# Byte offsets for fetched rows from VectorE, three tiles of five, and a run of 19 slices

## The chip, the cores and the metric

The kernel runs on one core of a Trainium2 chip. The metric is the device time of one execution in microseconds. A core has five engines that run their own instruction streams in order: TensorE (PE, whose weight loads the profile lists apart as PEld), VectorE (DVE), ScalarE (ACT), GpSimd (POOL) and SyncE (SP). They meet at semaphores. Sixteen DMA engines move data between the chip's memory (DRAM) and the on-chip buffers; in this kernel SP and POOL issue all transfers.

## The reference

A recommendation model: for each of 16384 samples, rows of tables are looked up and averaged, and three dense layers follow.

```
tok = word_emb[token_idx].mean(axis=1)          # 32 lookups in a 50000 x 300 table
e1 = emb_mh1[mh1_idx].mean(axis=1)              # 20 lookups each in tables of
e2 = emb_mh2[mh2_idx].mean(axis=1)              # 1000, 5000 and 10000 rows of 64
e3 = emb_mh3[mh3_idx].mean(axis=1)
o1, o2, o3, o4 = emb_oh1[oh1_idx], ...          # one lookup each, 100, 50, 20, 1000 rows
emb = concatenate([tok, e1, e2, e3, o1, o2, o3, o4], axis=1)
wide = sum of the looked-up rows of the seven width-1 tables
h = relu(emb @ W1 + b1)                         # 748 -> 1024
h = relu(h @ W2 + b2)                           # -> 512
h = relu(h @ W3 + b3)                           # -> 256
return sigmoid(h @ Wd + bd + wide)
```

All tensors are float32.

## The kernel before

**Tiles and steps.** The samples are cut into 128 tiles of 128 samples, one sample a partition. The program is one long list, written out by a loop over steps (lines 710 to 791): 11 steps a tile, and 27 more (`WAKE`) at the end, 1435 in all. In each step the loop issues a share of every kind of work, and each engine runs its own part of the list in the order in which it was issued. So the order of the work on every engine is fixed by hand; the engines only wait for each other's data and buffers.

**Small tables by counting.** The seven small tables (with their width-1 columns beside them) are not gathered. They stay on chip as 138 slices of 128 rows (`terms`): 8 for e1, 8 for o4, 40 for e2, 79 for e3 and one each for o1, o2, o3. For a tile, `one_hots` (line 387, DVE, then ACT) and `counts` (line 404, PE, then ACT) make a count of how often each sample names each row (`cnt`); the counts of tile t are made in the 11 steps of tile t. In the steps of the next tile, `small_sums` (line 427) multiplies each of the 138 slices of counts by its slice of the tables (line 447, PE). The fields go in pairs, (e1, o4), (e2, e3), (o1, o2) and (o3) alone: 16, 119, 2 and 1 slices. A pair's sums stand in the one bank `pg` (a pool with `bufs=1`, line 124), and a DVE reduction (line 437) empties it into the tile's features `g`. The next pair's first product waits for that reduction.

How many slices a step takes is a table made at lines 636 to 643. `early_sums` are issued ahead of the step's layer work, `late_sums` after it. Before the change they are 16 in step 1 (early), 20 in step 2 (late), 20 in each of steps 3 to 7 (early), 2 in step 9 (early) and 1 in step 10 (late). `run_sums` (line 647) draws that many from the generator, whatever pair they belong to, and `flush` (line 653) issues the reductions that have become due at the end of the step; a reduction of an early run is due in its own step, of a late run one step later. `sums_done` is the running total, and the layers are paced by how far it is from an even share (`ahead`, line 769).

**Word rows.** Each sample needs 32 rows of the word table, 1200 bytes each. `tokens` (line 285) issues an indirect gather on POOL for each of the 32 positions (line 300), two to a group, into one of six `tok_rows` buffers; three groups later `add_up` (line 272) adds both rows to a running sum on DVE (lines 276, 278 and 283). The groups are spread evenly over the steps, 1.42 groups (2.84 positions) a step after the first 24.

For some tiles the last of the 32 positions is not gathered by POOL. `load_column` (line 313) has SP load the tile's 128 indices of that position into one partition. `fetch` (line 320) has SP read them into its registers, 16 at a time (line 326), and issue one DMA a row (line 335), 128 rows a tile, into a buffer `fetched`, from which the last addition reads (line 283). Which tiles these are is line 679: every second one from tile 4. A fetch begins 24 steps before the step in which its tile is summed up (`FETCH_AHEAD`) and its rows are spread over 20 steps; the column is loaded 4 steps before that. `fetched` and `column` have two buffers each.

**Layers.** Two steps after a tile's features are complete they are transposed (line 488, PE; line 492, DVE) into `x`. Blocks of three tiles (two and one near the end) run through the three layers (line 565, PE; line 576, ACT) piece by piece within the steps, and the output is stored by SP (line 609).

**Order within a step**, as far as the change touches it: one-hots of the next step, counts, early sums, column loads and fetches, word-row groups, layers, late sums, then the reductions due.

Of the kernel before, what the change touches and what calls it, by code (L numbers as in the profile page):

```python
# [8 lines left out]
F32 = mybir.dt.float32  # L9
# [2 lines left out]
I32 = mybir.dt.int32  # L12
U32 = mybir.dt.uint32
U16 = mybir.dt.uint16
AF = mybir.ActivationFunctionType
ALU = mybir.AluOpType
AX = mybir.AxisListType

P = 128
N_TOK, TOK_D = 32, 300  # L20
# [7 lines left out]
FETCH_FROM = 4  # L28
FETCH_STEPS = 20
FETCH_AHEAD = 24  # L30
COLUMN_AHEAD = 4
LOADS = 16
WAKE = 27
EARLY = 3
BLOCK = 256
# [39 lines left out]
def kernel(  # L75
# [21 lines left out]
    nc = tc.nc  # L97
# [7 lines left out]
    for f in SMALL:  # L105
        n = -(-tables[f].shape[0] // P)
# [10 lines left out]
    fp = ctx.enter_context(tc.tile_pool(name="fetched", bufs=2))  # L117
# [54 lines left out]
    at = 0  # L172
# [27 lines left out]
    def convert_tables():  # L200
# [11 lines left out]
        def term(p, c):  # L212
            _, a, b = pieces[p]
            return terms[:, a:b, c * ROW : (c + 1) * ROW]

        def rows(p):
            k, a, b = pieces[p]
            return raws[k][:, a - parts[k] : b - parts[k], :]

        def make(p, c):  # L220

            if c == 0:
                nc.scalar.activation(term(p, 0), rows(p), AF.Copy, scale=COUNT)
                return
# [3 lines left out]
            for k in range(c):  # L228
                nc.tensor.matmul(left, minus_count, term(p, k), start=False, stop=(k == c - 1))
            nc.scalar.activation(term(p, c), left, AF.Copy, scale=COUNT)  # L230

# [77 lines left out]
            yield 1  # L309

    fetched, columns = {}, {}

    def load_column(t):

        columns[t] = fp.tile([1, P], I32, name="column")
        nc.sync.dma_start(
            out=columns[t], in_=idx[t * P : (t + 1) * P, N_TOK - 1 : N_TOK].rearrange("n o -> o n")
        )

    def fetch(t):  # L320


        rows = fp.tile([P, TOK_D], F32, name="fetched")
        column = columns.pop(t)
        for p0 in range(0, P, LOADS):
            _, values = nc.values_load_multi_w_load_instructions(
                column[:, p0 : p0 + LOADS],
                engines=[mybir.EngineType.SP],
                min_val=0,
                max_val=word.shape[0] - 1,  # L330
                skip_runtime_bounds_check_because="the indices are rows of the table",
            )
            for i, value in enumerate(values):
                p = p0 + i
                nc.sync.dma_start(out=rows[p : p + 1, :], in_=word[bass.ds(value, 1), :])  # L335
                if p == P - 1:
                    fetched[t] = rows
                yield 1

    def load_indices(blk):  # L340
# [46 lines left out]
    def one_hots(sc, s, i):  # L387
# [12 lines left out]
        upper = hot.rearrange("p (k w) n -> p k w n", w=2)[HALF:P, 0:rows, 0, 0:P]  # L400
        nc.scalar.activation(upper, upper, AF.Copy, scale=UPPER)  # L401
        return hot

    def counts(cnt, hot, i):
# [5 lines left out]
        for k in range(rows):  # L410
# [6 lines left out]
            pc[:, :, 0 : n * n_h].rearrange("l g (k h) -> l h g k", h=n_h),  # L417
            AF.Copy,
        )
# [122 lines left out]
    def flush_outputs():  # L542
        while pending:
            pending.pop(0)()
# [5 lines left out]
    def layer(dst, weights, bias, srcs, n_out, part=None):  # L550
# [3 lines left out]
        for m in range(n_out):  # L554
# [20 lines left out]
            def evict(m=m, ph=ph):  # L575
                nc.scalar.activation(dst[:, m, 0:n], ph[:, 0:n], AF.Relu, bias=bias[:, m : m + 1])  # L576

# [3 lines left out]
    def mlp(block, part=None):  # L581
# [20 lines left out]
        def finish():  # L602
            y = block.wide()
            nc.vector.tensor_add(y, po[:, 0:n].rearrange("o (a b) -> o a b", b=P), y)
            nc.scalar.activation(y, y, AF.Sigmoid, bias=bd_sb)
            b0 = block.first * P
# [29 lines left out]
    n_of = {f: slices[f][1] - slices[f][0] for f in SMALL}  # L636
    sizes_of_pairs = [sum(n_of[f] for f in SMALL[i : i + 2]) for i in (0, 2, 4, 6)]
    large = -(-sizes_of_pairs[1] // 6)
    early_sums = {1: sizes_of_pairs[0], 9: sizes_of_pairs[2], **{i: large for i in range(3, 8)}}
    late_sums = {2: large, 10: sizes_of_pairs[3]}  # L640
    sums_done = [0]
    for i in range(STEPS):
# [4 lines left out]
    def run_sums(gen, n, step, due):  # L647
        for _ in range(n):
            evict = next(gen, None)
            if evict:  # L650
                later.append((due, evict))
# [8 lines left out]
    tiles = B // P  # L660
    n_steps = tiles * STEPS + WAKE
    mlp_work = NK * M1 + M1 * M2 + M2 * M3 + M3
# [11 lines left out]
    def summed_at(t):  # L674

        n = n_groups * (t + 1) + TOK_LAG
        return n / FRONT_PACE if n < front else FRONT_STEPS + (n - front) / pace

    fetches = [(int(summed_at(t)) - FETCH_AHEAD, t) for t in range(FETCH_FROM, tiles, 2)]
    fetching = []  # L680

    def speed(step):

        left = n_steps - step
        return 1 / (TILE_STEPS if left > WAKE else TILE_STEPS_SUMS if left > STEPS + EARLY else TILE_STEPS_LAST)

# [6 lines left out]
    def block_for(t):  # L693
        if t not in block_of:
            n = ends[t] - t
            block = Block(t, n)
            block_of.update({t + k: block for k in range(n)})
        return block_of[t]
# [11 lines left out]
    for step in range(n_steps):  # L710
        t, i = divmod(step, STEPS)
        s = t % NSUB
        blk = t // NSUB + 1
        more = blk * NSUB < tiles
        if i == 0:
            sums = small_sums(t - 1, cnt) if 1 <= t <= tiles else None
            if t < tiles:
                if s == 0 and t:
                    sc = next_sc
                cnt = cp.tile([P, n_h, HALF], U16, name="cnt", tag="counts")  # L720
        if t < tiles:
            hot_now = hot
            if more and s == 0 and i == 0:
                ix = load_indices(blk)
            if more and s == 0 and i == 8:
                next_keys = lookup_keys(ix)
            if i < STEPS - 1:
                hot = one_hots(sc, s, i + 1)
            elif t + 1 < tiles:
                hot = one_hots(next_sc if s == NSUB - 1 else sc, (s + 1) % NSUB, 0)  # L730
            flush_outputs()
            counts(cnt, hot_now, i)
            tables_on_chip.to(TABLE_PACE * (step - 2))
            if t == 1 and i == STEPS - 1:
                load_weights()
        else:
            flush_outputs()
        if sums:
            run_sums(sums, early_sums.get(i, 0), step, step)
        outputs = list(rows_out)  # L740
        if waiting and step >= waiting[0][0]:
            _, k, ks = waiting[0]
            if k in summed or ks[0] < N_EARLY and k == tiles - 1:
                waiting.pop(0)
                block = block_for(k)
                later.append((step, block.transpose(k, ks)))
                if not block.missing:
                    complete.append(block)
        if complete and layers is None:
            flush(step)  # L750
            block = complete.pop(0)
            layers, target = start(block), 0
        for at, t_f in fetches:
            if step == at - COLUMN_AHEAD:
                load_column(t_f)
            if step == at:
                fetching.append((at, Paced(fetch(t_f))))
        for at, rows in list(fetching):
            rows.to(P * (step + 1 - at) / FETCH_STEPS)
            if step + 1 - at >= FETCH_STEPS:  # L760
                rows.finish()
                fetching.remove((at, rows))
        toks.to(tokens_by(step + 1))
        if t < tiles and more and s == 1 and i == (5 if t > 1 else 9):
            next_sc, evict = key_columns(next_keys)
            later.append((step, evict))
        ahead = 0
        if sums:
            ahead = n_h * (i + 1) / STEPS - sums_done[i + 1]
        if layers:  # L770
            target += mlp_work * LAYER_TIME * speed(step)
            layers.to(target + ahead)
            if layers.done >= layers.total:
                layers.finish()
                target -= layers.total
                layers = start(complete.pop(0)) if complete else None
        if sums:
            run_sums(sums, late_sums.get(i, 0), step, step + 1)
        flush(step)
        if outputs and rows_out[: len(outputs)] == outputs:  # L780
            flush_rows()
        flush_stores()
        if i == 0 and 2 <= t <= tiles + 1:
            wide_term(features(t - 2))
            if t - 2 < tiles - 1:
                waiting.append((step + 2, t - 2, range(NK)))
            else:
                waiting.append((step + 1, t - 2, range(N_EARLY)))
                waiting.append((step + 2, t - 2, range(N_EARLY, NK)))
        if step == n_steps - EARLY:  # L790
            part = early_part(block_of[tiles - 1])
# [49 lines left out]
```

## Time and profile before

| | us |
|---|---|
| runs: median (lowest to highest) | 5163.98 (5158.36 to 5164.18) |
| the profiled execution | 5157.98 |
| its span, first to last instruction | 5156.2 |
| PE busy | 4809.1 |
| POOL busy | 3819.6 |
| DVE busy | 3754.0 |
| ACT busy | 2757.7 |
| word gathers on POOL (line 300), 4034 | 3818.7 |
| slices on PE (line 447), 17664 | 1735.9 |
| reductions of `pg` on DVE (line 437), 512 | 262.1 |
| SP waiting for outputs to store (line 609), 51 times | 833.6 |

The profile is of one execution. Busy times are sums over an engine's instructions; register and DMA-issuing instructions count as busy on no engine, so SP has no busy share, and its load is read from the times between its instructions. Matmuls are pipelined, and their listed lengths overlap: the 17664 slices have a mean length of 248 ns, while 20 in a row take 1.9 us.

A line of groups gives the source line, the engine, the operation, what it writes and reads, and how often; then busy time and mean length; then how long the engine stood idle just ahead of it, and what ended that. A line of waits gives who waited for whom, the sum in us, how many times, and the longest. A line of the timeline gives the start in us, the length, engine and line, and in brackets the idle time before it with its releaser. "issue" means that nothing which the profile shows was waited for. A lane of DVE or ACT is one partition.

### The profile page before, as it was taken

To read this page: it belongs to the slowest core of one execution; us is meant where nothing else is said; L and a number is where in the kernel's file an instruction comes from. 1 tells how busy PE (TensorE), PEld (TensorE's weight loads), DVE (VectorE), ACT (ScalarE), POOL (GpSimd) and SP (SyncE) were. 2 spreads that over 40 slices of the span, in tenths; PEclk is the share of its full clock that TensorE was granted. 3 is DMA by queue.
4 is the path that set the end of the run, shared out by engine and by line. 5 is a ranking of instruction groups with operands and counts; after the bars stand their busy time and mean duration, and the time that the engine had idled before them with its cause. 6 is when DMAs were issued, how large, how long until landed. Compare 5 with 4: busy or idle time off the path is not lost.

```text
span 5156.2 us, 119649 instructions
## 1 busy us (share of the span) xinstructions
PE 4809.1 (93%) x36252; PEld 3716.6 (72%) x36252; DVE 3754.0 (73%) x6664; ACT 2757.7 (53%) x3658; POOL 3819.6 (74%) x4041
## 2 busy tenths in 40 slices
PE   6799999999999999999999999999999999999999
PEld 4566676676676667666667766766767888888898
DVE  6777777777777777777777777777777777777774
ACT  6455555555555555555555555555555555555552
POOL 7777777777777777777777777777777777777775
PEclk8899999999999999999999999999999999999999
DMA  7444444444444444444444444444444444444443
GB/s 202 128 126 126 123 127 127 124 126 124 125 127 123 124 127 124 125 126 125 125 125 126 125 126 123 127 128 127 127 128 124 126 125 124 128 127 127 127 120 100
DMA packets 276178, 653.78 MB, mean 127 GB/s; under 512 B 136091, under 2 KB 144667, under 8 KB 275527
## 3 DMA queue, kind: packets, MB, share of 16 engines
q0 software_dynamic: 193632, 619.88, 44.4%
q1 hardware_dynamic: 81895, 26.25, 2.4%
q8 instruction: 283, 4.64, 0.4%
q14 instruction: 368, 3.01, 0.2%
HBM read 645.63 MB, written 0.07 MB: 125 GB/s over the span
## 4 chain that ended last, share of the span: by engine, by line
PE 83%; DVE 9%; DMA 3%; issue 2%; ACT 2%; POOL 1%; SPq 1%; DVEq 0%; POOLq 0%; ACTq 0%
PE ph L565 44%; PE pg L447 28%; PE pc L412 8%; DMA tok_rows<-in_word_emb_dram,it 3%; DVE g L437 2%; DVE hot L394 2%; DVE own L278 2%; DVE own L283 2%; PE pc L488 2%; POOL tok_rows L300 1%; PE po L597 1%; DVE x L492 1%; ACT cnt L415 1%; ACT hot L401 0%; SPq L335 0%
## 5 line engine op out<-in xcount | busy, mean ns | idle before, releaser
L300 POOL DMA_INDIRECT tok_rows<-in_word_emb_dram,it x4034 | 3818.7, 947 | 1309.7 <-issue 907.9
L447 PE MATMUL pg<-terms,cnt 128*128 128x195 bf16 x17664 | 1735.9, 248 | 206.1 <-DVE g L437 206.1
L401 ACT ACTIVATE hot<-hot 64x768 bf16<-64x768 bf16 (+1 forms) x1408 | 1155.4, 821 | 1443.4 <-DVE hot L394 1427.5
L394 DVE TENSOR_TENSOR hot<-own,sc 128x1656 bf16<-128x1656 bf16 (+1 forms) x1408 | 1393.5, 990 | 367.9 <-PE pc L412 306.3
L447 PEld LDWEIGHTS <-cnt 128*128 128x128 fp8e3 x17664 | 1520.7, 98 | 43.2 <-issue 26.7
L565 PE MATMUL ph<-x,w_sb 128*128 128x384 f32 (+5 forms) x4932 | 1489.6, 441 | 45.8 <-DVE x L492 44.9
L415 ACT ACTIVATE cnt<-pc 128x828 uint16<-128x828 f32 (+1 forms) x1408 | 1186.9, 843 | 642.2 <-PE pc L412 615.0
L565 PE MATMUL ph<-h,w_sb 128*128 128x384 f32 (+2 forms) x4160 | 1219.6, 433 | 0.0
L565 PEld LDWEIGHTS ph<-x,w_sb 128*128 128x128 f32 (+1 forms) x4932 | 839.7, 192 | 454.9 <-issue 102.7
L278 DVE TENSOR_TENSOR own<-own,tok_rows 128x300 f32<-128x300 f32 x1920 | 917.5, 478 | 82.9 <-DMA tok_rows<-in_word_emb_dram,it 18.6
L565 PEld LDWEIGHTS ph<-h,w_sb 128*128 128x128 f32 x4160 | 700.4, 190 | 351.5 <-issue 103.8
L412 PEld LDWEIGHTS <-hot 128*128 128x128 bf16 x8192 | 592.0, 98 | 466.4 <-issue 220.7
L283 DVE TENSOR_TENSOR own<-own,tok_rows 128x300 f32<-128x300 f32 x1792 | 856.6, 478 | 94.3 <-DMA tok_rows<-in_word_emb_dram,it 33.3
L412 PE MATMUL pc<-hot 128*128 128x138 bf16 x8192 | 727.9, 224 | 55.8 <-ACT hot L401 53.5
L437 DVE TENSOR_REDUCE g<-pg 128x130 f32<-128x390 f32 (+1 forms) x512 | 262.1, 512 | 523.6 <-PE pg L447 518.2
L576 ACT ACTIVATE h<-ph,b_sb 128x384 f32<-128x384 f32 (+2 forms) x723 | 378.8, 524 | 274.6 <-PE ph L565 263.9
L492 DVE TENSOR_TENSOR x<-pc,scale 128x768 f32<-128x768 f32 x127 | 120.8, 951 | 105.8 <-PE pc L488 105.4
L381 DVE COPY sc<-pc 128x512 bf16<-128x512 bf16 x64 | 44.2, 691 | 144.4 <-PE pc L377 139.0
L488 PE MATMUL pc<-ident,g 128*128 128x128 f32 x762 | 106.7, 277 | 9.9 <-ACT cnt L415 9.9
L488 PEld LDWEIGHTS pc<-ident,g 128*128 128x128 f32 x762 | 83.0, 142 | 21.1 <-ACT cnt L415 16.8
L597 PE MATMUL po<-h,wd_sb 128*1 128x384 f32 (+2 forms) x208 | 70.0, 426 | 4.0 <-ACT h L576 2.7
L276 DVE TENSOR_TENSOR own<-tok_rows 128x300 f32<-128x300 f32 x128 | 61.3, 479 | 7.6 <-DMA tok_rows<-in_word_emb_dram,it 3.7
(54 smaller groups left out, 397.0 us busy)
## 6 DMA issues: line engine op xcount, KB each, us to landing
fetched<-in_word_emb_dram SPq DMA_DIRECT2D x7936, 1.2 KB
tok_rows<-in_word_emb_dram,it POOLq DMA_INDIRECT x4034
ix<-in_idx_dram SPq DMA_DIRECT2D x128, 32.0 KB
w_sb<-in_W_dram SPq DMA_DIRECT2D x6, 512.0 KB
raw<-in_mh_dram SPq DMA_DIRECT2D x4, 682.5 KB
it<-in_idx_dram SPq DMA_DIRECT2D x64, 32.0 KB
w_sb<-in_W_dram SPq DMA_DIRECT2D x1, 2048.0 KB
column<-in_idx_dram SPq DMA_DIRECT2D x62, 0.5 KB
```

The lines of the kernel that those rows point to most:

```text
L278: nc.vector.tensor_add(tok_sum, tok_sum, a)
L283: nc.vector.tensor_add(to, tok_sum, b)
L300: nc.gpsimd.indirect_dma_start(out=rows[-1], out_offset=None, in_=word, in_offset=bass.IndirectOffsetOnAxis(ap=it[:, j : j + 1], axis=0),)
L394: nc.vector.tensor_tensor(hot[:, 0 : 2 * rows, :].rearrange("p i (n d) -> p i n d", d=2), iota.rearrange("p (n d) -> p n d", d=2).unsqueez ...
L401: nc.scalar.activation(upper, upper, AF.Copy, scale=UPPER)
L412: nc.tensor.matmul(pc[:, k // n, at : at + n_h], hot[:, 2 * k, 0:P], hot[:, 2 * k + 1, :], start=True, stop=True)
L415: nc.scalar.activation(cnt[:, :, b : b + rows].rearrange("l h (g k) -> l h g k", g=2), pc[:, :, 0 : n * n_h].rearrange("l g (k h) -> l h g ...
L437: nc.vector.tensor_reduce(field_columns(features(t), pair), pg[:, 0:n, :].rearrange("p f (c d) -> p f d c", c=3), AX.X, ALU.add,)
L447: nc.tensor.matmul(pg[:, j, :], by_slice[:, h, :], terms[:, h, :], start=(h == h0), stop=(h == h1 - 1))
L488: nc.tensor.transpose(pt[:, j // n, j % n, :], g[:, c : c + P], ident)
L565: nc.tensor.matmul(to, weights[: src.shape[0], k, m * P : (m + 1) * P], src, start=(k == 0), stop=(k == len(srcs) - 1),)
L576: nc.scalar.activation(dst[:, m, 0:n], ph[:, 0:n], AF.Relu, bias=bias[:, m : m + 1])
```

## The change

Three things change.

1. The indices of a fetched column are turned into byte offsets on DVE. A new function `column_offsets` multiplies the 128 indices by 75 and shifts them left by 4 bits (together 1200, the bytes of a row), in place, one step before the fetch begins. The word table and the `fetched` buffer are seen as bytes, so the value that SP loads into a register is the offset of the DMA as it stands. According to the change's description SP then has one instruction a row.
2. The fetched tiles are those with t mod 5 equal to 0, 2 or 4, from tile 4 on: 75 tiles instead of 62.
3. The sixth run of the second pair (step 7) has 119 - 5 x 20 = 19 slices instead of 20. With that, step 9 holds o1 and o2, and step 10 holds o3, issued after the layers of that step, its reduction one step later.

```diff
+COLUMN_LAG = 1
 LOADS = 16
+ROW_BYTES = 4 * TOK_D
...
     fetched, columns = {}, {}
+    word_bytes = word.bitcast(U8).rearrange("n d -> (n d)").unsqueeze(0)
...
+    def column_offsets(t):
+
+
+        column = columns[t]
+        low = ROW_BYTES & -ROW_BYTES
+        nc.vector.tensor_single_scalar(column, column, ROW_BYTES // low, op=ALU.mult)
+        nc.vector.tensor_single_scalar(column, column, low.bit_length() - 1, op=ALU.logical_shift_left)
+
     def fetch(t):
...
-        rows = fp.tile([P, TOK_D], F32, name="fetched")
+        rows = fp.tile([P, TOK_D], F32, name="fetched").bitcast(U8)
...
-                max_val=word.shape[0] - 1,
+                max_val=(word.shape[0] - 1) * ROW_BYTES,
...
-                nc.sync.dma_start(out=rows[p : p + 1, :], in_=word[bass.ds(value, 1), :])
+                nc.sync.dma_start(out=rows[p : p + 1, :], in_=word_bytes[:, bass.ds(value, ROW_BYTES)])
                 if p == P - 1:
-                    fetched[t] = rows
+                    fetched[t] = rows.bitcast(F32)
...
-    early_sums = {1: sizes_of_pairs[0], 9: sizes_of_pairs[2], **{i: large for i in range(3, 8)}}
+    early_sums = {1: sizes_of_pairs[0], 9: sizes_of_pairs[2], **{i: large for i in range(3, 7)}}
+    early_sums[7] = sizes_of_pairs[1] - 5 * large
...
-    fetches = [(int(summed_at(t)) - FETCH_AHEAD, t) for t in range(FETCH_FROM, tiles, 2)]
+    fetches = [(int(summed_at(t)) - FETCH_AHEAD, t) for t in range(FETCH_FROM, tiles) if t % 5 % 2 == 0]
...
         for at, t_f in fetches:
             if step == at - COLUMN_AHEAD:
                 load_column(t_f)
+            if step == at - COLUMN_LAG:
+                column_offsets(t_f)
             if step == at:
                 fetching.append((at, Paced(fetch(t_f))))
```

More of the change, by code (lines that the diff above doesn't have):

```diff
@@ L14 @@
 U16 = mybir.dt.uint16
+U8 = mybir.dt.uint8
 AF = mybir.ActivationFunctionType
```

## The prediction

> **What bounds the kernel now.** I read the busy shares first, then what TensorE (PE) waits for, then the gathers' group on GpSimd (POOL), then the timeline of one tile.
>
> The page's first part and its two largest groups:
>
> ```profile
> PE 4809.1 (93%) x36252; PEld 3716.6 (72%) x36252; DVE 3754.0 (73%) x6664; ACT 2757.7 (53%) x3658; POOL 3819.6 (74%) x4041
> L300 POOL DMA_INDIRECT tok_rows<-in_word_emb_dram,it x4034 | 3818.7, 947 | 1309.7 <-issue 907.9
> L447 PE MATMUL pg<-terms,cnt 128*128 128x195 bf16 x17664 | 1735.9, 248 | 206.1 <-DVE g L437 206.1
> ```
>
> Waits of all engines, longest in total first (us in total, times, longest), with those of PE and one of POOL:
>
> ```profile
> PE pg L447 <- DVE g L437: 206.1, 259, 6.2
> POOL tok_rows L300 <- DVE own L283: 169.1, 327, 3.0
> ...
> PE pc L412 <- ACT hot L401: 53.5, 51, 3.3
> PE ph L565 <- DVE x L492: 44.9, 38, 2.6
> ```
>
> PE is busy 4809 us, and all its waits sum to about 341 us: together the span. PE does nothing else, and 206 us of its waiting is for one thing, the reduction that empties the one `pg` bank. Sorted by the slice's place within its tile (138 slices a tile), these waits are two a tile, 128 times each: before slice 135 (96.3 us) and before slice 137 (108.3 us), plus 1.5 us at slice 16.
>
> The timeline around step 7 and around step 9 of a tile:
>
> ```profile
> 2535.60 1.80 PE L447 MATMUL pg<-terms,cnt 128*128 128x195 bf16 x19
> 2537.43 0.56 DVE L437 TENSOR_REDUCE g<-pg 128x130 f32<-128x390 f32 x1 [0.90 <-PE pg L447]
> 2538.05 0.24 PE L447 MATMUL pg<-terms,cnt 128*128 128x195 bf16 x1 [0.65 <-DVE g L437]
> ```
>
> ```profile
> 2503.62 0.24 PE L447 MATMUL pg<-terms,cnt 128*128 128x195 bf16 x1
> 2503.91 0.57 DVE L437 TENSOR_REDUCE g<-pg 128x130 f32<-128x390 f32 x1 [0.21 <-PE pg L447]
> 2504.53 0.24 PE L447 MATMUL pg<-terms,cnt 128*128 128x195 bf16 x1 [0.66 <-DVE g L437]
> 2504.81 0.36 DVE L437 TENSOR_REDUCE g<-pg 128x65 f32<-128x195 f32 x1 [0.34 <-PE pg L447]
> ```
>
> The run of step 7 has 20 slices, the pair (e2, e3) only 19 left: the 20th, o1 of the next pair, stands still until the bank is emptied. In step 9 o2 closes the third pair and o3 comes straight behind it: the same stop again.
>
> The second bound is POOL, whose gathers in the timeline look like this:
>
> ```profile
> 2341.16 0.95 POOL L300 DMA_INDIRECT tok_rows<-in_word_emb_dram,it  x1 [0.30 <-issue]
> 2342.41 0.95 POOL L300 DMA_INDIRECT tok_rows<-in_word_emb_dram,it  x1 [0.30 <-issue]
> 2345.44 0.95 POOL L300 DMA_INDIRECT tok_rows<-in_word_emb_dram,it  x1 [2.08 <-DVE own L276]
> ```
>
> 0.95 us plus a pause of 0.30 us, a gather every 1.25 us, with nothing between. The first starts at 3.0 us, the last at 5128.9 us; 4033 periods of 1.25 us are 5041 us of these 5126. Of the 85 us over, 79 us are 109 pauses over 0.32 us, in which POOL waits for a `tok_rows` buffer that VectorE (DVE) gives back late, most often at step 8 of a tile, right behind the stop of step 7. So PE is ahead of POOL as the bound by 79 us and no more.
>
> SyncE (SP) issues the fetched rows:
>
> ```profile
> L335 SPq FUSED_REGOPS  x7936: 37/37/51, 109.0 to 5074.4; - x199
> L335 SPq MOVE fetched<-in_word_emb_dram x7936: 29/29/39, 109.1 to 5074.5; - x199
> L335 SPq DMA_DIRECT2D fetched<-in_word_emb_dram x7936: 217/224/311, 109.1 to 5074.5; - x199
> L326 SPq TENSOR_LOAD <-column x496: 1138/1232/1492, 107.5 to 5067.0; - x166
> ```
>
> Three instructions a row, 408 ns from row to row with the gaps, and a 1.33 us load of registers (gaps included) for 16 rows: 62.9 us a tile, 62 x 62.9 = 3900 us, 76% of the span.
>
> [...] 62 gathers that overlap L363 (`ix`, SBUF to SBUF, 128 int32 a lane) took 951 ns in the mean against 946. [...] 224 ns of record, while the row's packet ends 1.17 us (median) after the issue. [...] The clock records of this run show 13 pieces of 3.41 us at half clock between 300 and 5150 us[...].
>
> **The change, part by part.**
>
> *Slices.* 16 + 6 x 20 reached into the third pair; now the sixth run stops at 135, step 9 has o1 and o2, and step 10 has o3 behind its layers. The stop at slice 135 goes (96.3 us). The one at 137 should go too (108.3 us): between o2 and o3 there are now the layers of step 9 (1.5 us of PE), the counts of step 10 and its layers, over 3 us against 0.57 us of reduction. What could be late next: the reduction of o3 now runs at step 0 of the next tile, ahead of the 16 slices of step 1, which need its bank. In the timeline at 2313 to 2316 us, DVE ends step 0's additions at 2315.0 and PE starts the 16 slices at 2315.99; 0.36 us fits between. I take 0, with 0.66 us x 128 = 84 us as the other end. The layers' pacing moves by 1 slice unit in two steps, below a tenth of a layer matmul: nothing.
>
> *Tiles fetched.* Every second from 4 gives 62; those with t mod 5 in {0, 2, 4} give 75. 13 gathers fewer: 13 x 1.25 = 16.3 us of POOL. Additions stay as many.
>
> *SP.* One instruction a row leaves 224 ns and a gap of about 50: 275 ns. A tile costs 128 x 0.275 + 8 x 1.33 = 45.8 us, and 75 tiles 3437 us (67%), less than now. The other end is 408 ns as now. Where it is tight is the pair of adjacent tiles (4 and 5, 9 and 10): the second one's first register load waits for DVE, which writes the offsets one step before that fetch, so SP stands there until DVE has come that far, with some 58 of the first tile's rows behind it. From there to the first tile's last row are 116 rows, 7 loads (9.6 us), index loads and a store (2.7 us): 31.9 + 12.3 = 44 us, and 1.3 us to land. The use comes some 14.3 steps on, at 3.5 us 50 us. It fits by 5 us. Rows of `fetched` are now issued 17 us or more before their use.
>
> *Offsets on DVE.* Two int32 operations of 128 elements, nearest rows L362 and L363 with 247 and 261 ns: 150 x 0.25 = 38 us in all, in DVE's 27% idle; nothing on the path, 38 us at most. They wait for the column's load. Behind them on DVE stand additions, then the next `hot`, so PE and POOL would feel it. But SP now issues the column so early that it has landed 12 to 44 us before DVE reaches that point; with one step's less work on SP this does not shrink much. 0. [...]
>
> *What is left.* Over six tiles (66 steps) PE has 222.3 us of work and 13 us of waits, 8.5 of them for `pg` (medians of the matmul records between `hot` number k and k + 66): 235.5 us. POOL needs 66 x 2.839 - 2.9 = 184.5 gathers, 230.6 us. Afterwards PE needs 222.3 + 4.6 = 227 us, POOL 183.9 x 1.25 = 229.9 us. The bound passes to POOL, and of PE's 205 us only the part down to POOL's pace is seen. Sum: 5156.2 - 16.3 - 79.3 = 5060.6 us if POOL never stands. PE's room is only 1.3%, so some pauses will stay: I take 8 us, between 0 and 30. Between 3200 and 3800 us POOL has only 0.5 us of such pauses even now, which speaks for a small number. Span 5068.6; the profiled execution has 5157.98 us for 5156.2 of span, so 5070.4. The median of the runs shown is 6.0 us above that execution: 5076. As a run bound by POOL should scatter less, I say 5074.
>
> **Rivals.**
> *A stop remains (B).* The wait before o3 or before the next tile's first slice takes the place of one removed. PE then needs 227 + 6 x 0.8 = 232 us for six tiles, 2 us over POOL; 21 times that is 42 us: about 5115. For it: the bank is still single, and PE and DVE are often within 1 us of each other. Against: the other instructions put between.
> *SP comes too late (C, slower).* If a row keeps costing 408 ns (the issue itself being the limit, or the landing of the DMA eight before on the same semaphore), the pair of adjacent tiles needs 116 x 0.408 + 13.6 = 61 us where 50 are there. DVE, in order, stands 11 us at the last addition of the first tile, with `hot` and so PE behind it; up to 7.5 us are covered by the three groups that POOL is ahead. 25 pairs x 3.5 to 11 us = 90 to 275 us on top of 5074: near 5240. It starts to bite between 0.31 and 0.38 us a row and eats the whole gain at about 0.41. Against it: after a plain DMA on SP the next instruction starts 0.04 to 0.05 us later in the loads of the weights, and eight rows at 0.275 are 2.2 us, more than a landing takes (1.3 to 2.1 us).
> *The gathers alone (D).* If DVE or the hand-over between layer blocks holds POOL as before, only 16 us come: 5148. Against: the pauses follow the stop of step 7.
>
> **Chances.** POOL bound, as forecast: 0.72. B 0.12, D 0.03, C 0.13. The range 5055 to 5130 takes in 0 to 30 us of pauses, the scatter of the runs and B, and leaves out C and D. Faster by over 0.2% (what a measurement of this kernel can tell from no change) 0.84, within 0.2% 0.03, slower 0.13.
>
> **What would show it.** Right: L447 waits for L437 almost nothing; 4021 gathers, with less than 30 us of pauses over 0.32 us; PE's waits pass to `hot` and `own`, and `own` waits more for the gathers' DMA; rows of SP about 0.275 us apart; no long wait of L283 for `fetched`. Wrong: waits of DVE for `fetched` or `column`, or `pg` waits at slice 0 or 137.

## The result and the profile after

| | before | after |
|---|---|---|
| median of 6 runs each, us (lowest to highest) | 5160.08 (5158.36 to 5164.18) | 5067.03 (5066.49 to 5068.49) |
| ratio, with its 95% interval | | 0.9819 (0.9806 to 0.9831) |
| the profiled execution, us | 5157.98 | 5068.49 |
| its span, us | 5156.2 | 5066.7 |
| last gather starts at, us | 5128.9 | 5034.2 |
| from there to the end of the span, us | 27.3 | 32.5 |

The kernel became 1.8% faster, 93 us. Where the kernel before stands at 7378 to 7461 us in what follows, and not at about 5160, both kernels ran in a slower state, which one chip showed at one time and not at another (7379 and 5159 us for the kernel before) and in which PE pauses for no cause that the profile shows (558 us ahead of the slices in the first run below), so a ratio from there says nothing of the bound of a run of 5160 us.

All lines of the code have moved: the slices are now line 459, their reduction 449, the gathers 303, the additions 279 to 286, the fetched rows 347, their register loads 338, the offsets 329 and 330, the transposes 500 and the layers 577.

The page's busy shares and two groups, after (columns as before):

```profile
PE 4811.1 (95%) x36252; PEld 3731.2 (74%) x36252; DVE 3748.8 (74%) x6814; ACT 2739.9 (54%) x3658; POOL 3807.6 (75%) x4028
...
L303 POOL DMA_INDIRECT tok_rows<-in_word_emb_dram,it x4021 | 3806.7, 947 | 1226.9 <-issue 784.0
...
L459 PE MATMUL pg<-terms,cnt 128*128 128x195 bf16 x17664 | 1723.6, 249 | 35.5 <-DVE g L449 35.5
```

The work is what it was; PE's 4811 us now stand in a shorter span. The slices' wait for the bank fell from 206.1 to 35.5 us. None is left ahead of slice 135, three (5.3 us) ahead of slice 137; 26.5 us in 23 waits stand at a place that had none before, the first slice of a tile.

The gathers show the new bound: 4021 of them, the first at 2.98 us, the last at 5034.16, and no pause over 0.32 us anywhere. 4020 periods of 1.2515 us are these 5031 us. POOL never waits for a buffer longer than its usual pause, although its busy share is 75%. Behind the run of step 7, where the pauses were most frequent before, and in the sum of one of its waits (the last number is the longest):

```profile
2559.40 0.95 POOL L303 DMA_INDIRECT tok_rows<-in_word_emb_dram,it  x1 [0.30 <-issue]
2560.65 0.95 POOL L303 DMA_INDIRECT tok_rows<-in_word_emb_dram,it  x1 [0.30 <-issue]
2561.90 0.95 POOL L303 DMA_INDIRECT tok_rows<-in_word_emb_dram,it  x1 [0.30 <-DVE own L286]
...
POOL tok_rows L303 <- DVE own L286: 196.0, 643, 0.3
```

The waits of all engines, after (who waited for whom: sum in us, times, longest):

```profile
DVE own L286 <- DMA tok_rows<-in_word_emb_dram,it: 327.2, 509, 2.9
...
DVE own L281 <- DMA tok_rows<-in_word_emb_dram,it: 178.3, 247, 3.1
...
PE pc L424 <- ACT hot L413: 81.4, 60, 4.5
...
PE pg L459 <- DVE g L449: 35.5, 29, 2.7
...
DVE g L286 <- DMA fetched<-in_word_emb_dram: 12.5, 10, 3.5
```

Read from the top: DVE now waits some 550 us (with 44.2 us of line 279) for gathered rows, where it waited 56 us. It has caught up with the gathers, as an engine behind the bound does. PE's wait for `hot`, which DVE and ACT make, rose from 53.5 to 81.4 us. In 45 of these 60 waits (63.5 us) DVE had stood for gathered rows in the 6 us before, against 12 of 51 before the change: DVE stood in its additions, so `hot` came later. PE's idle time fell from 347 us (5156.2 - 4809.1) to 256 us; the slices' waits fell by 171 us, so some 80 us of the freed time came back as other waits.

The two places of a tile where PE stood, after:

```profile
2557.20 1.80 PE L459 MATMUL pg<-terms,cnt 128*128 128x195 bf16 x19
2559.03 0.56 DVE L449 TENSOR_REDUCE g<-pg 128x130 f32<-128x390 f32 x1 [0.91 <-PE pg L459]
...
2563.51 0.33 PE L459 MATMUL pg<-terms,cnt 128*128 128x195 bf16 x2
2564.03 0.56 DVE L449 TENSOR_REDUCE g<-pg 128x130 f32<-128x390 f32 x1
```

19 slices and no 20th behind them; o1 and o2 as a pair of their own, with no o3 on their heels. No slice line carries a wait in brackets.

SP's rows by line 347, a MOVE and a DMA each (durations as lowest/median/highest in ns, first and last start in us), after:

```profile
L347 SPq MOVE fetched<-in_word_emb_dram x9600: 29/29/43, 117.4 to 5017.0; - x196
L347 SPq DMA_DIRECT2D fetched<-in_word_emb_dram x9600: 217/225/391, 117.5 to 5017.0; - x196
```

There are two instructions a row, and not one: only the FUSED_REGOPS have gone, the MOVE has stayed. Row follows row at a median of 320 ns (before 408).

SP has a new wait as well. Its first register load of a column (line 338) stands until DVE has written the offsets, which DVE does in its order, behind additions. These are 75 waits, one a column, 727 us in all, and in the median the load starts 27 ns behind the offsets' end. The profile puts most of them down to an addition:

```profile
SPq L338 <- DVE own L286: 664.0, 66, 27.5
```

Before the change the same loads waited some 10 us in all, none of it for DVE.

### The profile page after: what moved, and what is told of

Its sections match the earlier page's. It is cut to its first block, busy times and chain, and to the rows that moved or that the text cites. A ratio compares the mean times of both kernels' runs of the same rounds, so it can differ in the third digit from the quotient of the medians.

```text
span 5066.7 us, 115364 instructions
## 1 busy us (share of the span) xinstructions
PE 4811.1 (95%) x36252; PEld 3731.2 (74%) x36252; DVE 3748.8 (74%) x6814; ACT 2739.9 (54%) x3658; POOL 3807.6 (75%) x4028
## 4 chain that ended last, share of the span: by engine, by line
PE 58%; DMA 14%; DVE 11%; issue 8%; POOL 4%; SPq 2%; ACT 1%; DVEq 0%; POOLq 0%; ACTq 0%
PE ph L577 31%; PE pg L459 20%; DMA tok_rows<-in_word_emb_dram,it 14%; PE pc L424 6%; POOL tok_rows L303 4%; DVE hot L406 4%; DVE own L286 3%; DVE own L281 2%; SPq L347 2%; PE pc L500 1%; DVE x L504 1%; ACT hot L413 1%; DVE g L449 1%; SPq L338 1%; ACT cnt L427 0%
## 5 line engine op out<-in xcount | busy, mean ns | idle before, releaser
L459 PE MATMUL pg<-terms,cnt 128*128 128x195 bf16 x17664 | 1723.6, 249 | 35.5 <-DVE g L449 35.5
L577 PE MATMUL ph<-x,w_sb 128*128 128x384 f32 (+5 forms) x4932 | 1506.4, 444 | 63.7 <-DVE x L504 53.6
L424 PE MATMUL pc<-hot 128*128 128x138 bf16 x8192 | 729.5, 225 | 90.8 <-ACT hot L413 81.4
L279 DVE TENSOR_TENSOR own<-tok_rows 128x300 f32<-128x300 f32 x128 | 61.4, 480 | 47.2 <-DMA tok_rows<-in_word_emb_dram,it 44.2
L500 PEld LDWEIGHTS pc<-ident,g 128*128 128x128 f32 x762 | 84.1, 143 | 15.5 <-ACT cnt L427 14.3
```

Source lines behind the costliest of these rows:

```text
L424: nc.tensor.matmul(pc[:, k // n, at : at + n_h], hot[:, 2 * k, 0:P], hot[:, 2 * k + 1, :], start=True, stop=True)
L459: nc.tensor.matmul(pg[:, j, :], by_slice[:, h, :], terms[:, h, :], start=(h == h0), stop=(h == h1 - 1))
L500: nc.tensor.transpose(pt[:, j // n, j % n, :], g[:, c : c + P], ident)
L577: nc.tensor.matmul(to, weights[: src.shape[0], k, m * P : (m + 1) * P], src, start=(k == 0), stop=(k == len(srcs) - 1),)
```

## The experiments

Each experiment's time stands beside that of the kernel before, measured with it.

### The slices alone

```diff
-    early_sums = {1: sizes_of_pairs[0], 9: sizes_of_pairs[2], **{i: large for i in range(3, 8)}}
+    early_sums = {1: sizes_of_pairs[0], 9: sizes_of_pairs[2], **{i: large for i in range(3, 7)}}
+    early_sums[7] = sizes_of_pairs[1] - 5 * large
```

This is the kernel before with the third part of the change only.

> The kernel before with the sixth run of the second pair at 19 slices, and nothing else: 62 fetched tiles, three SP instructions a row, 4034 gathers. Two-bound theory (PE's two stops a tile held POOL; without them POOL's 1.25 us a gather sets the time): the changed kernel's 5067 plus 13 gathers of 1.25 us, 5083 to 5087 us, no POOL pause over 0.32 us, pg waits at slices 135 and 137 gone. Rival (the gathers taken off POOL brought the gain): at most 20 us below before, 5140 to 5160 us.

7301.37 us against 7378.30: 0.9885 (0.9862 to 0.9908). The same kernel, measured again:

> The same kernel as e1_slices_alone (19 slices in the sixth run, nothing else changed; 62 tiles, old rows), for a chip on which the kernel before takes about 5160 us as in its own profile; on the chip of the first four runs it took 7378 us, with PE standing still for microseconds that no other engine explains. Two-bound theory: 5083 to 5087 us if before is 5160 (ratio 0.985), no POOL pause over 0.32 us. Rival (the gathers taken off POOL brought the gain): 5140 to 5160 us (ratio 0.997 and more). If PE stands still here too: ratio near the 0.9885 of the first run, and nothing learnt on the bound.

5082.25 us (5081.59 to 5082.91) against 5158.85: 0.985 (0.983 to 0.9869). That is 0.75 us under the low end of what was forecast for the POOL bound, and far from the rival's 5140. All 4034 gathers come without a pause over 0.32 us, the last at 5048.45 us, 80.4 us earlier than before, where 79.3 us of pauses were to go. One of POOL's waits, with 0.3 us as its longest:

```profile
POOL tok_rows L300 <- DVE own L283: 196.6, 645, 0.3
```

The waits at slice 135 have gone, those at 137 are 6.0 us, those at a tile's first slice 25.3 us. This edit of the table alone brings 77 of the 93 us.

### The fetching alone

```diff
-    early_sums = {1: sizes_of_pairs[0], 9: sizes_of_pairs[2], **{i: large for i in range(3, 7)}}
-    early_sums[7] = sizes_of_pairs[1] - 5 * large
+    early_sums = {1: sizes_of_pairs[0], 9: sizes_of_pairs[2], **{i: large for i in range(3, 8)}}
```

This is the kernel after with the old table of slices: byte offsets and 75 tiles, both stops back.

> The changed kernel with the run of 20 slices put back: byte offsets and 75 fetched tiles stay. Two-bound theory: PE stays the bound with its 205 us of pg waits, the 13 gathers less only lengthen POOL's pauses (79 us to about 95 us): 5150 to 5160 us. Rival (the gathers brought the gain): 5067 to 5085 us.

7347.65 us against 7378.30: 0.9953 (0.9935 to 0.9971). Measured again:

> The same kernel as e2_fetch_alone (byte offsets and 75 tiles, but the run of 20 slices put back), again for a chip on which before takes about 5160 us. Two-bound theory: PE stays the bound with about 205 us of pg waits at slices 135 and 137, POOL's pauses grow from 79 to about 95 us: 5150 to 5160 us (ratio 0.998 to 1.000). Rival: 5067 to 5085 us (ratio 0.982 to 0.985).

5172.20 us (11 runs, 5167.28 to 5179.39) against 5158.85: 1.0023 (1.0014 to 1.0032). Slower by 13 us, and outside the 5150 to 5160 us that were expected. Two of its waits:

```profile
PE pg L459 <- DVE g L449: 211.7, 259, 7.0
POOL tok_rows L303 <- DVE own L286: 196.0, 342, 3.8
```

Both stops are back (94.4 and 115.8 us). POOL's pauses are 108 us in place of 79: the 16.3 us of the 13 gathers left out turned into pauses, and the last gather came 14 us later on top. While PE is the bound, fewer gathers bring nothing; that part of the theory holds. The 14 us were not foreseen. Set tile against tile (from the first slice of one to that of the next), the 72 tiles in which one column's two offset instructions run differ from before by 0.00 us in the median: no cost of the offsets shows even here. 11.6 of the 14 us lie between the first slices of the first and the last tile, and 6.2 of these in the nine tiles in which DVE waited for fetched rows, 5.7 in two of them. The longest such wait, in the timeline:

```profile
1015.09 0.47 DVE L286 TENSOR_TENSOR g<-own,fetched 128x300 f32<-128x300 f32 x1 [2.86 <-DMA fetched<-in_word_emb_dram]
```

The other 5.4 us come from a dozen tiles, most of them 1.5 to 1.7 us longer or shorter than before, more of them longer. That is half of 3.41 us, the length of each of the 13 pieces at half clock between 300 and 5000 us before; here the clock records show 64.8 us at half clock in that stretch, 44.4 before. By these numbers an estimate of 10 us, half of the 20 more, could be the clock's, in part in the same tiles as the waits for rows. Why there were more such pieces was not tested, so the cause of the 13 us stays open.

### 75 tiles with the old rows

```diff
-    fetches = [(int(summed_at(t)) - FETCH_AHEAD, t) for t in range(FETCH_FROM, tiles, 2)]
+    fetches = [(int(summed_at(t)) - FETCH_AHEAD, t) for t in range(FETCH_FROM, tiles) if t % 5 % 2 == 0]
```

This is the kernel before with this edit and the new table of slices of the first experiment; the rows stay at three instructions and 408 ns, with no offsets on DVE. It is rival C made real.

> 19 slices and 75 fetched tiles, but the rows issued as before: no offsets on DVE, three SP instructions and about 0.408 us a row. Theory that SP's time a row decides in the pairs of adjacent tiles: the first tile of each of 25 pairs comes some 10 us later than in the changed kernel, where ten of them were already waited for (12.5 us in all); 7.5 us of each are covered by what POOL is ahead; DVE waits for fetched 150 to 250 us in all, time 5100 to 5270 us. Rival (the lead of 24 steps hides SP whatever a row costs): 5067 to 5072 us.

7626.53 us against 7378.30: 1.0336 (1.0318 to 1.0353).

> 19 slices and 75 tiles with rows issued as before (no offsets on DVE, three SP instructions, 0.408 us a row). For a chip on which before takes about 5160 us; on the first chip, where everything took 7378 us, this form was the slowest, 7627. Theory that SP's time a row decides in the pairs of adjacent tiles: DVE waits for fetched at most of the 25 pairs, 150 to 250 us in all, against 12.5 us in the changed kernel; POOL's pauses come back; 5100 to 5270 us. Rival (the lead of 24 steps hides it, the first chip's loss was its own): 5065 to 5072 us.

7762.58 us against 7460.81: 1.0401 (1.0362 to 1.044). Once more:

> 19 slices and 75 tiles with rows issued as before (no offsets on DVE, three SP instructions, 0.408 us a row), for a chip on which before takes about 5160 us; on the chip where before took 7380 to 7460 us this form was 3 to 4% slower than before, with DVE waiting for fetched at most pairs. Theory that SP's time a row decides in the pairs of adjacent tiles: DVE waits for fetched 100 to 250 us in all against 12.5 us in the changed kernel, POOL's pauses come back, 5085 to 5270 us. Rival (the lead of 24 steps hides it where SP does not stand still of itself): 5065 to 5072 us.

5162.68 us (11 runs, 5159.84 to 5163.82) against 5162.87: 0.9999 (0.999 to 1.0009). The whole gain is gone, with both stops gone too (6.3 us left at slice 137). Its waits and one place of its timeline:

```profile
DVE g L283 <- DMA fetched<-in_word_emb_dram: 269.3, 41, 14.0
```

```profile
2391.20 48.88 SPq L335 DMA_DIRECT2D fetched<-in_word_emb_dram  x98
```

```profile
2413.92 0.95 POOL L300 DMA_INDIRECT tok_rows<-in_word_emb_dram,it  x1 [0.30 <-issue]
2419.32 0.94 POOL L300 DMA_INDIRECT tok_rows<-in_word_emb_dram,it  x1 [4.46 <-DVE own L276]
```

```profile
2415.93 0.47 DVE L283 TENSOR_TENSOR g<-own,fetched 128x300 f32<-128x300 f32 x1 [13.17 <-DMA fetched<-in_word_emb_dram]
```

SP issues row after row with no rest, DVE stands 13.17 us for the last of them with the additions queued behind, and POOL, six buffers ahead, stands for 4.46 us. Summed over the run, DVE's standing of 269 us goes with 94 us of POOL's pauses, 72 us of these within 20 us behind such a wait, and the pauses are the loss: without them the last gather would have come at 5034 us, where the changed kernel has it at 5034.2. What the new table gains is kept only if the rows come in time.

### The last slice straight behind its neighbours

```diff
-    early_sums = {1: sizes_of_pairs[0], 9: sizes_of_pairs[2], **{i: large for i in range(3, 7)}}
+    early_sums = {1: sizes_of_pairs[0], 9: sizes_of_pairs[2] + sizes_of_pairs[3], **{i: large for i in range(3, 7)}}
...
-    late_sums = {2: large, 10: sizes_of_pairs[3]}
+    late_sums = {2: large}
```

The kernel after with one of the two stops, the one before slice 137, put back.

> The changed kernel with o3 put back into step 9 behind o1 and o2, so that only the stop before slice 137 comes back. Theory that the two stops add up and that PE has 1.3% of room over POOL: about 108 us of pg waits, PE needs 232 us for six tiles against POOL's 229.9: about 5105 us, between 5085 and 5125. Rival (one stop removed was enough, POOL hides the other): 5066 to 5072 us.

7285.64 us against 7378.30: 0.9869 (0.9852 to 0.9886).

> The changed kernel with o3 put back into step 9 behind o1 and o2: the stop before slice 137 alone comes back, some 108 us of pg waits. For a chip on which before takes about 5160 us. Theory that the stops add up on PE and PE has 1.3% of room over POOL: PE needs 232 us for six tiles against POOL's 229.9: 5085 to 5125 us. Rival (with one stop gone POOL hides the other): 5066 to 5072 us.

7375.20 us against 7460.81: 0.9884 (0.9841 to 0.9926). With the kernel before at over 7300 us both times, this does not tell whether a single stop would have left PE under POOL's pace, and so cost nothing; it stays open.

### The end of the run

The table above has 5.2 us more behind the last gather than before. PE's timeline there, after:

```profile
5038.16 0.90 PE L500 MATMUL pt<-ident,g 128*128 128x128 f32 x3 [6.85 <-DVE g L286]
5039.71 2.50 PE L577 MATMUL pc<-x,w_sb 109*128 109x128 f32 x10 [0.65 <-DVE x L504]
```

The same two groups before:

```profile
5133.29 0.55 PE L488 MATMUL pt<-ident,g 128*128 128x128 f32 x3 [1.82 <-DVE g L283]
5134.49 1.38 PE L565 MATMUL pc<-x,w_sb 109*128 109x128 f32 x10 [0.65 <-DVE x L492]
```

Behind an idle time of 6.85 us the same ten matmuls take 2.50 us, not 1.38; the granted clock is a half for 17 us from 5033.8 on. From these transposes to the end are 28.5 us, before 22.9. PE had run out of other work earlier, being faster than the gathers on which the last tile depends. The run with the slices alone has the same end, with 32.0 us behind its last gather:

```profile
5051.89 0.91 PE L488 MATMUL pt<-ident,g 128*128 128x128 f32 x3 [7.55 <-DVE g L283]
5053.44 2.51 PE L565 MATMUL pc<-x,w_sb 109*128 109x128 f32 x10 [0.65 <-DVE x L492]
```

To try it, matmuls that nothing reads fill this idle time:

```diff
+    idle = ps_h.tile([P, N], F32, name="idle", tag="ph")
+    for k in range(16):
+        nc.tensor.matmul(idle.rearrange("p (a b) -> p a b", b=P), w1_sb[:, 0, 0:P], x_ring[:, 0:LAYER_TILES, 0, :], start=True, stop=True)
     for _, k, ks in waiting:
         block = block_for(k)
         block.transpose(k, ks)()
```

> The changed kernel with 16 matmuls of 128x384 f32 on PE, ahead of the last tile's second transposes, whose output is read by nobody: they fill the 6.9 us in which PE waits there for the last word rows. In the changed kernel the last gather starts at 5034.2 us, where the kernel before left POOL's floor, and yet 32.5 us follow it, against 27.3 us before; from 5033.8 us on the clock record is at half for 17 us. Theory that this half clock costs the last block about 5 us: 5060 to 5064 us where the changed kernel takes 5067, with about 28 us behind the last gather. Rival (the tail is longer for another reason): 5066 to 5074 us.

7293.84 us against 7383.74: 0.9874 (0.9839 to 0.9909), which says nothing of 5 us in 5067. Its trace does show the end: the 16 matmuls took 10.5 us, the ten matmuls behind them 1.38 us again, and from the last transposes to the end were 23.4 us, where the changed kernel has 28.5.

### More tiles, with room, and a warm end

```diff
-FETCH_AHEAD = 24
+FETCH_AHEAD = 30
...
-    fetches = [(int(summed_at(t)) - FETCH_AHEAD, t) for t in range(FETCH_FROM, tiles) if t % 5 % 2 == 0]
+    fetches = [(int(summed_at(t)) - FETCH_AHEAD, t) for t in range(FETCH_FROM, tiles) if t % 3]
...
+    idle = ps_h.tile([P, N], F32, name="idle", tag="ph")
+    for k in range(10):
+        nc.tensor.matmul(idle.rearrange("p (a b) -> p a b", b=P), w1_sb[:, 0, 0:P], x_ring[:, 0:LAYER_TILES, 0, :], start=True, stop=True)
```

The kernel after, with 83 tiles fetched (two of three), a lead of 30 steps, and ten filling matmuls.

> The changed kernel with 10 of the filling matmuls in the tail (16 took 10.5 us, more than the 6.9 us to be filled) and with two tiles of three fetched (83), a fetch beginning 30 steps ahead instead of 24, so that SP's rows come sooner. For a chip on which before takes about 5160 us. Theory: POOL is the bound with 4013 gathers, 8 fewer, 10 us; the tail gives back about 5 us; the changed kernel's 5067 becomes 5050 to 5056 us. Rival (PE's 1.3% of room is used up, or SP comes too late with 83 tiles): POOL's pauses come back and the time is 5060 us or more. On a chip where PE and SP stand still of themselves the ratio to before says nothing on it.

7304.67 us against 7379.23: 0.9894 (0.9869 to 0.9918). Measured again:

> The same kernel as g6_warm_two_of_three (83 tiles fetched, 30 steps ahead; 10 filling matmuls in the tail), for a chip on which before takes about 5160 us. Theory: POOL is the bound with 4013 gathers and no pauses, 10 us less; the tail gives back about 5 us: 5050 to 5056 us. Rival (PE's 1.3% of room is used up, or SP comes too late): POOL's pauses come back, 5060 us or more.

5052.18 us (5051.57 to 5052.48) against 5158.84: 0.9791 (0.9775 to 0.9808). Its end on PE, in the timeline:

```profile
5019.71 6.62 PE L813 MATMUL idle<-x,w_sb 128*128 128x384 f32 x20
5026.47 0.52 PE L500 MATMUL pt<-ident,g 128*128 128x128 f32 x3
5027.64 1.38 PE L577 MATMUL pc<-x,w_sb 109*128 109x128 f32 x10 [0.65 <-DVE x L504]
```

4013 gathers without a pause, the last at 5022.37 us, 11.8 us earlier than after (8 gathers of 1.25 us are 10.0, and a mean period 0.4 ns shorter is the rest), and 27.2 us behind it where after has 32.5. These two parts, 11.8 and 5.3 us, are the whole difference of the spans, 5066.7 - 5049.6. Two waits for fetched rows are left, together 0.5 us. Its runs lie below every run of the changed kernel; the two were not timed side by side, and their ratios to the kernel before just touch.

## Why the prediction was right, and where it was not

5074 was forecast and 5067 measured, inside the range of 5055 to 5130. By its steps:

*Both stops go, and nothing takes their place.* Right for the time, though the second half is not quite so. One of rival B's two cases did appear, at a tile's first slice, as 23 waits of 26.5 us together and not as 128 of 0.66 us each. It was on the prediction's list of signs of being wrong; POOL, being the bound, had no pause all the same. The experiment with the slices alone shows this part by itself: 79 us of pauses forecast, 80 us found.

*13 gathers are 16.3 us.* Right in size, and only because the stops went: with them the same gathers brought nothing (the fetching alone). Between the slices alone and the full change the last gather moved by 14.3 us; a gather's mean period is 0.5 ns longer, which is the 1.9 us between.

*The bound passes to POOL.* Right. From one `hot` on DVE to the 66th behind it are 230.2 us in the median after, 235.4 before; 229.9 was worked out for POOL, 227 for PE.

*Pauses of 8 us.* There were none, the low end of the term. PE's room of 1.3% was enough, with the six buffers between DVE and POOL.

*The end of the run.* Missing in the sum. The idle window ahead of the last transposes grew to 6.85 us, and behind it PE ran at half clock: 5.2 us more. The prediction spoke of half clock for the middle of the run only. In the trace the clock is halved within the 6.85 us, some 2.5 us after the last matmul, and it is not halved in the 1.82 us of before; with the window filled, the ten matmuls behind it took 1.38 us again and not 2.50. With no pauses and this end the sum closes: span 5060.6, no pauses, 5.2 us of the end, 0.9 us for the gathers' spacing, is 5066.7. That the forecast span of 5068.6 lies so near is in part luck: 8 us that did not come stood against 6 that were not in the sum. The other 5 us between 5074 and 5067 lie between profile and median. The forecast put the median 3.6 us above the profiled execution, from three runs of the kernel before of which two took 5164 us (over six runs its median is 5160.08, 2.1 us above its profile); after the change the profiled execution was the highest of six, 1.5 us above the median. That the runs would scatter less came true: 2.0 us from the lowest to the highest of six, 5.8 before.

*One instruction a row, 275 ns.* This step failed. A register MOVE of 29 ns in the median remains ahead of each of the 9600 DMAs, and rows stand 320 ns apart. The pair of adjacent tiles then needs 116 x 0.320 + 12.3 + 1.3 = 51 us by the prediction's own sum (where seven loads of 1.33 us are 9.3 us, not 9.6), and the 5 us of room in its 50 us are gone. The 50 us were too many as well: in the 25 pairs, DVE came to the first tile's last addition 42.7 to 51.3 us behind the second tile's offsets, 46.6 in the median. Hence ten waits for fetched rows, 12.5 us, eight of them in the tiles with t mod 5 = 4, the first of a pair. In these eight the rows were there 43.8 to 48.2 us behind the offsets, so the 51 us are too many too. The waits were another of the listed signs of being wrong, and POOL's lead hid them all; that this step did no harm was a margin which the prediction had not counted on.

The estimate of where rows begin to bite (0.31 to 0.38 us) and where they eat the whole gain (about 0.41) agrees with the two points on record: at 0.320 us DVE waits now and then, at 0.408 us the gain was gone. The price put on that case, near 5240 us, was too high: measured were 5163, 96 us over the changed kernel, where 90 to 275 us were allowed for.

*Offsets on DVE at nothing.* Right for DVE's and PE's time. 204 and 216 ns each in the median, 34 us in all, where 38 were taken; in the median no tile is longer for them, even where PE is the bound. SP does wait for them, 727 us, which the prediction foresaw for the pairs. The 87 gathers that overlap them took 947.2 ns in the mean, the others 946.7. So no cost of the offsets shows on POOL's gathers either.

*Rival D* (only the 16 us of the gathers come) is refuted by the slices alone. *Rival C* is real, but begins beyond the rows of this change: with 75 tiles, the instruction that was taken away, 37 ns and the gaps with it, is what kept the gain.

Not shown: the byte offsets with 62 tiles, one of the two stops by itself beside a kernel before of 5160 us, and old rows with a longer lead.

## What to carry to other kernels

A second bound that stands 80 us under the first caps what the removal of a 206 us wait can bring. Work out the next bound's own floor (number of instructions times their period) and forecast that. A saving on an engine that is not the bound turns into its pauses, so the 13 gathers were worth 14 us together with the new table and nothing without it. Where two tiles' transfers follow each other without rest, reckon the issue per row against the lead of the pair, not against the whole span: by an estimate from the measured durations SP issued for 75 x (128 x 0.320 + 8 x 1.33) = 3870 us, three quarters of the span, and was late now and then all the same. Work handed from a full engine to an idle one also ties the two: SP's loads now stand for DVE's offsets, 727 us in all.

## What was not expected of the hardware

- The 9600 row DMAs after the change take the byte offset from the register as it stands, and the trace still shows a MOVE ahead of each, 29 ns in the median; 320 ns from row to row, not the 225 ns of the DMA and a gap of 50.
- The idle time of PE at the end of this run was paid twice. Behind 6.85 us without a matmul came the end of the run at half clock, 17 us of it: ten matmuls took 2.50 us for 1.38, and 5 us of the run were lost. Ten matmuls that nothing reads (20 in the trace), 6.62 us in that same idle time, gave it back.
- PE spent more time at half clock where it was not the bound: between 300 and 5000 us 44.4 us before, 99.0 after, 122.9 with the slices alone, and 204.8 in the run with the old rows and 75 tiles. After, POOL had no pause, so none of this reached the time ahead of the last gather.
